# Gathering the whole-array TensorE work of an attention loop in two places per unit, with an earlier start and a mask loaded in pieces

## The chip, the core and the metric

The kernel runs on one core of a Trainium2 chip, in fp32, as one launch. The metric is the time of one execution in microseconds (us), measured on the device. Engine names: PE is TensorE's matmul queue, PEld its weight loads, DVE is VectorE, ACT ScalarE, POOL GpSimd, SP the queue that issues transfers.

## The reference, cut to what matters

```python
def _L0_gnn_ref(features, A, ...):              # a graph layer over 2048 nodes
    A_hat = (A + I) * dinv[:, None] * dinv[None, :]
    agg = einsum('nm,bmd->bnd', A_hat, features)
    h   = relu(batchnorm(agg @ W1.T + b1))
    return batchnorm(h @ W2.T + b2)
def _L1_gnn_ref(h, W, adj):                     # masked attention, 4 heads of 64
    q, k, v = split(h @ W)
    scores  = q @ k.T / sqrt(64) + where(adj == 0, -inf, 0)
    return softmax(scores) @ v
x = layernorm(x + _L0_gnn_ref(x, adj, ...))     # x is (8, 2048, 256)
x = layernorm(x + _L1_gnn_ref(x, W, adj))
```

## The kernel before

Everything up to the second linear layer (1423 us) stays as it is, except for the place of two loads. The change is in attention, which is organised in 64 *units*: 8 batches, 2 pairs of heads, 4 chunks of 512 query rows. A unit has 8 *steps*. In each step a score group S and a weighing group W run:

```python
def scores(u, g):                       # S: 4 matmuls, each on 64 of the 128 rows
    for j in range(g * GJ, (g + 1) * GJ):
        ps = ps_s.tile([P, 2, CH], F32, name="ps_s")         # pool of 2 buffers
        for h in range(2):
            nc.tensor.matmul(ps[:, h, :], kt[hs, ...], qt[hs, ...], ...)
    for j in ...:
        pt = ap_.tile([P, 2, CH], F32, name="pt", bufs=10)
        nc.vector.tensor_tensor(pt, ps, mask[...], op=ALU.subtract)  # frees ps_s
        nc.scalar.activation(pt, pt, AF.Exp, scale=2.0**MASK_EXP)
        nc.gpsimd.tensor_add(acc, acc, pt)                   # sums of the softmax
def weigh(u, g):                        # W: 4 matmuls, each on 64 of the columns
    nc.tensor.matmul(outs[u][h * HD : (h + 1) * HD, :], v[...], pt[:, h, :], ...)
```

About S: its two buffers come free only when DVE has subtracted the mask.

Beside S and W there is *whole-array* work, on all 128 rows and columns: transposes of y and x, the projections to q, k and v, and the transposes that finish a unit. Their results share a pool of two buffers, `ps_m`. There are two layer norms per chunk and batch, one for the input of attention (`prep_norm`) and one for the output (`emit`). Both use this function:

```python
def layernorm(t):
    for i in range(TPC):
        nc.vector.bn_stats(st[:, i, :], t[:, i, :])
        nc.vector.bn_aggr(mv[:, i, :], st[:, i, :])
    nc.vector.tensor_scalar(rs, mv[:, :, 1], EPS, None, op0=ALU.add)      # DVE
    nc.gpsimd.tensor_tensor(rs, rs, mhalf[:, :TPC], op=ALU.pow)           # POOL
    nc.vector.scalar_tensor_tensor(                                       # DVE
        nm, mv[:, :, 0], -1.0, rs, op0=ALU.mult, op1=ALU.mult)
    for i in range(TPC):
        nc.scalar.activation(t[:, i, :], t[:, i, :], AF.Identity,
                             bias=nm[:, i : i + 1], scale=rs[:, i : i + 1])
```

DVE works in order. Between its second-last and its last operation here it has to wait for POOL, which has a queue of 128x1024 additions of its own.

The steps of the whole-array work are set by a table `side`; S and W come from the loop:

```python
for g in range(total + NG):
    scores(g)
    side[(g, 0)]
    weigh(g - LAG)                      # LAG = 2
    side[(g, 1)]
```

This order is not yet the order of the queue: a scheduler may move instructions among each other by its own estimates, unless an instruction is held with `tc.keep_in_program_order`.

Of the kernel before, what the change touches and what calls it, by code (L numbers as in the profile page):

```python
# [8 lines left out]
F32 = mybir.dt.float32  # L9
# [19 lines left out]
def tile_gcn_then_masked_attention(  # L29
# [15 lines left out]
    nc = tc.nc  # L45
    PSUM = bass.MemoryType.PSUM
    P = 128
    B, N, D = x.shape
# [3 lines left out]
    NT = N // P  # L52
    ND = D // P
    NH = H // P
    NO = O // P
    CH = 512
    NCH = N // CH
# [14 lines left out]
    mask_d = dram.tile([P, NT, N], U8, name="mask_d")  # L72
# [21 lines left out]
    with ExitStack() as kept:  # L94
# [182 lines left out]
        with tc.tile_pool(name="l0b", bufs=3) as lp, tc.tile_pool(  # L277
            name="psy", bufs=4, space=PSUM
        ) as psy:
            for i in range(NALL):  # L280
                h = hp_.tile([P, NH, CH], F32, name="h")
                nc.sync.dma_start(h, h_d[i])
                if i == 4:
                    nc.sync.dma_start(wq, wqkv.rearrange("(c p) f -> p c f", p=P))
                    nc.sync.dma_start(mask, mask_d)
                for f in range(NH):
                    nc.scalar.activation(  # L287
                        h[:, f, :], h[:, f, :], AF.Relu,
                        bias=sh1[:, f : f + 1], scale=sc1[:, f : f + 1],
                    )  # L290
                y = lp.tile([P, NO, CH], F32, name="y")
                for o in range(NO):
                    py = psy.tile([P, CH], F32, name="py")
                    for f in range(NH):
                        nc.tensor.matmul(  # L295
                            py,
                            w2s[:, f, o * P : (o + 1) * P],
                            h[:, f, :],
                            start=(f == 0),
                            stop=(f == NH - 1),  # L300
                        )
                    nc.vector.tensor_scalar(y[:, o, :], py, b2s[:, o : o + 1], None, op0=ALU.add)
                    nc.vector.bn_stats(st2[:, o, i, :], y[:, o, :])
                nc.sync.dma_start(y_d[i], y)
            batchnorm_affine(lp, st2, NO, g2s, be2s, sc2, sh2, "2")
# [4 lines left out]
def attention(tc, x, out, adj, mask, wq, ident, ones, mhalf, sc2, sh2, sall, y_d, x1_d):  # L310
# [16 lines left out]
    with ExitStack() as ctx:  # L327
# [28 lines left out]
            return src[b, k * CH : (k + 1) * CH, :].rearrange("(t p) d -> p t d", p=P)  # L356

        def prep_load(b, k):
            yt[b, k] = ap_.tile([P, NO, CH], F32, name="yt")
            nc.sync.dma_start(yt[b, k], y_d[b * NCH + k])  # L360
            x1[b, k] = ap_.tile([P, TPC, D], F32, name="x1", bufs=7)
            nc.sync.dma_start(x1[b, k], rows(b, k, x))
# [20 lines left out]
        def prep_norm(b, k):  # L383
            yt.pop((b, k))
            layernorm(x1[b, k])
            r0 = b * N + k * CH
            nc.sync.dma_start(
                x1_d[r0 : r0 + CH, :].rearrange("(t p) d -> p t d", p=P), x1[b, k]
            )
# [10 lines left out]
        def project(b, hp, c, which):  # L400

            if (b, hp) not in qkv:
                qkv[b, hp] = (
                    ap_.tile([P, N], F32, name="qt"),
                    ap_.tile([P, N], F32, name="kt"),
                    ap_.tile([P, NT, P], F32, name="v"),
                )
            xt = x1t[b]
            cols = slice(c * CH, (c + 1) * CH)
            wcols = slice(which * D + hp * P, which * D + (hp + 1) * P)  # L410
            pm = ps_m.tile([P, CH], F32, name="pm")
            if which < 2:
                for d in range(ND):
                    nc.tensor.matmul(  # L414
                        pm, wq[:, d, wcols], xt[:, d, cols], start=(d == 0), stop=(d == ND - 1)
                    )
                scale = HD**-0.5 * 2.0**-MASK_EXP if which == 0 else 1.0
                nc.scalar.activation(qkv[b, hp][which][:, cols], pm, AF.Copy, scale=scale)
            else:
                for j in range(TPC):  # L420
                    t = c * TPC + j
                    for d in range(ND):
                        nc.tensor.matmul(
                            pm[:, j * P : (j + 1) * P],
                            xt[:, d, t * P : (t + 1) * P],
                            wq[:, d, wcols],
                            start=(d == 0),
                            stop=(d == ND - 1),
                        )
                nc.scalar.copy(  # L430
                    qkv[b, hp][2][:, c * TPC : (c + 1) * TPC, :].rearrange("p t d -> p (t d)"), pm
                )
# [95 lines left out]
                nc.sync.dma_start(rows(b, k, out), t)  # L528


        per_b = HP * NCH * NG
        side = {}

        def at_step(g, s, f, *args):
            side.setdefault((g, s), []).append((f, args))

        def prep_at(b, k, g):
            at_step(g - 6, 0, prep_load, b, k)
            at_step(g - 2, 1, prep_bn, b, k)
            at_step(g, 0, prep_res, b, k, 0)  # L540
            at_step(g, 1, prep_res, b, k, 1)
            at_step(g, 1, prep_norm, b, k)
            for d in range(ND):
                at_step(g + 4, d, prep_t, b, k, d)

        for b in range(B):
            g0 = b * per_b
            for c in range(NCH):
                for w in range(3):
                    at_step(g0 + 3 + 3 * c + w, 1, project, b, 1, c, w)  # L550
            if b + 1 < B:
                for k, g in enumerate((17, 23, 29, 48)):
                    prep_at(b + 1, k, g0 + g)
                for c, g in enumerate((35, 41, 47, 54)):
                    for w in range(3):
                        at_step(g0 + g + 2 * w, 1, project, b + 1, 0, c, w)
        for u in range(len(units)):
            g0 = (u + 1) * NG
            at_step(g0 + 1, 1, finish_copy, u)
            at_step(g0 + 4, 0, finish_sums, u)  # L560
            at_step(g0 + 5, 0, finish, u)
            at_step(g0 + 5, 1, emit, u)

        for k in range(NCH):
            prep_load(0, k)
            prep_bn(0, k)
            for half in range(2):
                prep_res(0, k, half)
            prep_norm(0, k)
            for d in range(ND):  # L570
                prep_t(0, k, d)
            for w in range(3):
                project(0, 0, k, w)

        total = len(units) * NG
        LAG = 2
        for g in range(total + NG):
            if g < total:
                scores(*divmod(g, NG))
            for f, args in side.get((g, 0), ()):  # L580
                f(*args)
            if 0 <= g - LAG < total:
                weigh(*divmod(g - LAG, NG))
            for f, args in side.get((g, 1), ()):
                f(*args)


# [207 lines left out]
```

## Time and profile before

| | before |
|---|---|
| time, median of three executions | 4072.41 us (4071.86 to 4076.46) |
| busy share of PE, DVE, ACT, POOL | 97%, 46%, 41%, 56% |
| first y-transpose to last matmul | 1423.1 to 4066.2 us |
| a steady batch of attention | 324 us |

### The profile page before, as it was taken

What the parts mean: (1) busy time and instruction counts of PE and PEld (TensorE: products, weight loads), DVE (VectorE), ACT (ScalarE), POOL (GpSimd) and SP (SyncE); (2) the same over time, 40 slices, a digit from 0 to 9 for tenths busy, and PEclk for the clock granted to TensorE, in tenths of its full rate; (3) what the DMA queues carried; (4) which work ended last, traced back from release to release, by engine and by line L of the source; (5) the groups of instructions that cost most, each with busy time, mean ns of one, the idle gap of its engine ahead of it and who ended that gap; (6) DMA issues with size and microseconds to landing.
All of it is one profiled execution on the core that took longest, in us unless ns stands there. A gap on an engine that the chain in (4) does not pass through costs nothing. (4 is left out here: it accounts for less than half of the span.)

```text
span 4072.3 us, 38096 instructions
## 1 busy us (share of the span) xinstructions
PE 3938.3 (97%) x14626; PEld 1559.8 (38%) x14626; DVE 1867.2 (46%) x2525; ACT 1665.7 (41%) x2077; POOL 2285.9 (56%) x1083
## 2 busy tenths in 40 slices
PE   7999999999989989999999999999999999999997
PEld 5444444444434433333333333333333333333332
DVE  5211111111124435665565665665656666556565
ACT  5000000000024345555555555555555555545554
POOL 0011101110100038887887887888888888788897
PEclk8999999999999989999999999999999999999998
DMA  5111101110147620000010000000000000000000
GB/s 217 64 45 52 52 31 49 47 49 31 47 158 230 208 68 21 25 28 26 16 42 21 21 32 21 32 32 21 32 21 32 26 27 27 26 6 26 6 1 22
DMA packets 94426, 197.28 MB, mean 48 GB/s; under 512 B 7072, under 2 KB 73120, under 8 KB 83872
## 3 DMA queue, kind: packets, MB, share of 16 engines
q1 hardware_dynamic: 94240, 194.80, 13.7%
q8 instruction: 117, 1.92, 0.2%
q14 instruction: 69, 0.57, 0.0%
HBM read 106.70 MB, written 88.08 MB: 48 GB/s over the span
## 5 line engine op out<-in xcount | busy, mean ns | idle before, releaser
L466 POOL TENSOR_TENSOR acc<-acc,pt 128x1024 f32<-128x1024 f32 x768 | 1814.2, 2362 | 329.1 <-ACT pt L459 286.5
L453 DVE TENSOR_TENSOR pt<-ps_s,mask 128x1024 f32<-128x1024 f32 x1024 | 1209.4, 1217 | 943.5 <-PE ps_s L446 908.4
L459 ACT ACTIVATE pt<-pt 128x1024 f32<-128x1024 f32 x1024 | 1066.5, 1054 | 816.7 <-DVE pt L453 796.2
L446 PE MATMUL ps_s<-qt,kt 64*128 64x512 f32 x4096 | 1041.1, 620 | 47.8 <-DVE pt L453 47.7
L475 PE MATMUL ps_o<-pt,v 128*64 128x512 f32 x4096 | 1013.0, 607 | 2.9 <-ACT pt L459 2.9
L209 PE MATMUL pa<-at,xb 128*128 128x512 f32 x2048 | 885.5, 592 | 0.0
L446 PEld LDWEIGHTS ps_s<-qt,kt 64*128 64x128 f32 x4096 | 351.3, 186 | 640.1 <-issue 339.9
L187 POOL TENSOR_SCALAR xb<-xb,dinv 128x256 f32<-128x256 f32 x112 | 103.0, 948 | 863.9 <-DMA xb<-in_x_dram 851.8
L209 PEld LDWEIGHTS pa<-at,xb 128*128 128x128 f32 x2048 | 389.0, 190 | 487.2 <-issue 480.0
L475 PEld LDWEIGHTS ps_o<-pt,v 128*64 128x64 f32 x4096 | 252.0, 136 | 637.6 <-issue 539.8
L242 ACT ACTIVATE h<-ph,b1s 128x512 f32<-128x512 f32 x128 | 87.9, 687 | 993.9 <-PE ph L235 993.9
L228 DVE TENSOR_TENSOR ag<-pa,dbc 128x512 f32<-128x512 f32 x64 | 44.3, 692 | 769.8 <-PE pa L209 769.8
L464 POOL TENSOR_TENSOR acc<-pt 128x1024 f32<-128x1024 f32 x128 | 302.3, 2362 | 71.4 <-ACT pt L459 70.2
L414 PE MATMUL pm<-x1t,wq 128*128 128x512 f32 x512 | 255.7, 624 | 0.5 <-ACT x1t L398 0.5
L295 PE MATMUL py<-h,w2s 128*128 128x512 f32 x512 | 223.6, 599 | 13.7 <-ACT h L287 13.7
L235 PE MATMUL ph<-ag,w1s 128*128 128x512 f32 x512 | 225.1, 592 | 0.0
L88 POOL TENSOR_TENSOR rs<-rs,mhalf 128x4 f32<-128x4 f32 (+1 forms) x2 | 1.7, 870 | 378.9 <-DVE rs L87 378.9
L350 ACT ACTIVATE x<-x,ln_nm,ln_rs 128x256 f32<-128x256 f32 x256 | 132.6, 588 | 100.0 <-DVE ln_nm L346 100.0
L243 DVE BATCH_NORM_STATS2 st<-h 128x6 f32<-128x512 f32 x128 | 88.8, 694 | 148.5 <-ACT h L242 148.5
L414 PEld LDWEIGHTS pm<-x1t,wq 128*128 128x128 f32 x512 | 88.4, 191 | 165.7 <-issue 104.9
L295 PEld LDWEIGHTS py<-h,w2s 128*128 128x128 f32 x512 | 98.4, 193 | 138.9 <-issue 119.1
L287 ACT ACTIVATE h<-h,sh,sc 128x512 f32<-128x512 f32 x128 | 93.3, 801 | 134.9 <-DMA h<-h_d 125.3
(78 smaller groups left out, 1780.7 us busy)
## 6 DMA issues: line engine op xcount, KB each, us to landing
h_d<-h SPq DMA_DIRECT2D x32, 1024.0 KB, 3.9
h<-h_d SPq DMA_DIRECT2D x32, 1024.0 KB, 5.9
a<-in_adj_dram SPq DMA_DIRECT2D x16, 1024.0 KB, 8.3
xb<-in_x_dram SPq DMA_DIRECT2D x32, 512.0 KB, 3.9
y_d<-y SPq DMA_DIRECT2D x32, 512.0 KB, 6.4
yt<-y_d SPq DMA_DIRECT2D x32, 512.0 KB, 3.3
x<-in_x_dram SPq DMA_DIRECT2D x32, 512.0 KB, 3.8
x_d<-x SPq DMA_DIRECT2D x32, 512.0 KB, 2.8
```

The source lines that it names most:

```text
L187: nc.gpsimd.tensor_scalar(t4[:, j, :], t4[:, j, :], dv, None, op0=ALU.mult)
L209: nc.tensor.matmul(pa, xs[b][m // TPC][:, m % TPC, d * P : (d + 1) * P], at[:, m, c * CH : (c + 1) * CH], start=(m == 0), stop=(m == NT - 1),)
L235: nc.tensor.matmul(ph, w1s[:, d, f * P : (f + 1) * P], ag[:, d, :], start=(d == 0), stop=(d == ND - 1),)
L295: nc.tensor.matmul(py, w2s[:, f, o * P : (o + 1) * P], h[:, f, :], start=(f == 0), stop=(f == NH - 1),)
L350: nc.scalar.activation(t[:, i, :], t[:, i, :], AF.Identity, bias=nm[:, i : i + 1], scale=rs[:, i : i + 1],)
L414: nc.tensor.matmul(pm, wq[:, d, wcols], xt[:, d, cols], start=(d == 0), stop=(d == ND - 1))
L446: nc.tensor.matmul(ps[:, h, :], kt[hs, j * P : (j + 1) * P], qt[hs, k * CH : (k + 1) * CH], start=True, stop=True,)
L453: nc.vector.tensor_tensor(pt, pss[j - g * GJ], mask[:, j, None, k * CH : (k + 1) * CH].to_broadcast([P, 2, CH]), op=ALU.subtract,)
L459: nc.scalar.activation(pt, pt, AF.Exp, scale=2.0**MASK_EXP)
L464: nc.gpsimd.tensor_add(accs[u, q], probs[u, j - 1], pt)
L466: nc.gpsimd.tensor_add(accs[u, q], accs[u, q], pt)
L475: nc.tensor.matmul(outs[u][h * HD : (h + 1) * HD, :], qkv[b, hp][2][:, j, h * HD : (h + 1) * HD], pt[:, h, :], start=(j == 0), stop=(j == ...
```

## The change

A change of the array's shape costs time (0.15 to 0.20 us here, measured in the prediction), and before, whole-array work stands in 366 places of the matmul queue, for 512 steps. The change puts all of it at two steps of each unit, 2 and 5. It also starts the first unit after the first chunk is ready instead of after all four, and loads the mask in 16 pieces. The core of the diff (cuts marked with `...`):

```diff
-                if i == 4:
+                if i == 2:
                     nc.sync.dma_start(wq, ...)
-                    nc.sync.dma_start(mask, mask_d)
+                if 4 <= i < 4 + NT:
+                    nc.sync.dma_start(mask[:, i - 4, :], mask_d[:, i - 4, :])
...
-            yt[b, k] = ap_.tile([P, NO, CH], F32, name="yt")
+            yt[b, k] = ap_.tile([P, NO, CH], F32, name="yt", bufs=3)
...
-                for w in range(3):
-                    at_step(g0 + 3 + 3 * c + w, 1, project, b, 1, c, w)
-            if b + 1 < B:
-                for k, g in enumerate((17, 23, 29, 48)):
-                    prep_at(b + 1, k, g0 + g)
-                for c, g in enumerate((35, 41, 47, 54)):
-                    for w in range(3):
-                        at_step(g0 + g + 2 * w, 1, project, b + 1, 0, c, w)
+                u0 = g0 + c * per_u
+                if b or c:
+                    for w, g in enumerate((2, 2, 5)):
+                        at_step(u0 + g, project, b, 1, c, w)
+                if b + 1 < B:
+                    u0 = g0 + (NCH + c) * per_u
+                    prep_at(b + 1, c, u0 - 3, u0 + 2)
+                    for w, g in enumerate((2, 2, 5)):
+                        at_step(u0 + g, project, b + 1, 0, c, w)
...
+        first_rows(0)
+        first_rows(1)
+        prep_load(0, 3)
+        first_columns(0)
+        at_step(0, first_rows, 2)
+        at_step(1, first_columns, 1)
+        at_step(2, first_rows, 3)
+        at_step(3, first_columns, 2)
+        at_step(5, first_columns, 3)
...
             if g < total:
                 scores(*divmod(g, NG))
-            for f, args in side.get((g, 0), ()):
-                f(*args)
             if 0 <= g - LAG < total:
                 weigh(*divmod(g - LAG, NG))
-            for f, args in side.get((g, 1), ()):
+            for f, args in side.get(g, ()):
                 f(*args)
```

`prep_at(b + 1, c, u0 - 3, ...)` puts the input layer norm at step 5 of the unit before, the same step at which `finish` and `emit` (the output layer norm) stand.

More of the change, by code (lines that the diff above doesn't have):

```diff
@@ L528, in emit, with at_step, prep_at @@
                 nc.sync.dma_start(rows(b, k, out), t)
+        per_u = NG
         per_b = HP * NCH * NG
         side = {}
-        def at_step(g, s, f, *args):
-            side.setdefault((g, s), []).append((f, args))
-        def prep_at(b, k, g):
-            at_step(g - 6, 0, prep_load, b, k)
-            at_step(g - 2, 1, prep_bn, b, k)
-            at_step(g, 0, prep_res, b, k, 0)
-            at_step(g, 1, prep_res, b, k, 1)
-            at_step(g, 1, prep_norm, b, k)
+        def at_step(g, f, *args):
+            side.setdefault(g, []).append((f, args))
+        def prep_at(b, k, g, t):
+            at_step(g - 6, prep_load, b, k)
+            at_step(g - 2, prep_bn, b, k)
+            for half in range(2):
+                at_step(g, prep_res, b, k, half)
+            at_step(g, prep_norm, b, k)
             for d in range(ND):
-                at_step(g + 4, d, prep_t, b, k, d)
+                at_step(t, prep_t, b, k, d)
         for b in range(B):
@@ L548, in attention, with first_rows @@
             for c in range(NCH):
-                for w in range(3):
-                    at_step(g0 + 3 + 3 * c + w, 1, project, b, 1, c, w)
-            if b + 1 < B:
-                for k, g in enumerate((17, 23, 29, 48)):
-                    prep_at(b + 1, k, g0 + g)
-                for c, g in enumerate((35, 41, 47, 54)):
-                    for w in range(3):
-                        at_step(g0 + g + 2 * w, 1, project, b + 1, 0, c, w)
+                u0 = g0 + c * per_u
[7 more added lines that the diff above has]
+                        at_step(u0 + g, project, b + 1, 0, c, w)
         for u in range(len(units)):
             g0 = (u + 1) * NG
-            at_step(g0 + 1, 1, finish_copy, u)
-            at_step(g0 + 4, 0, finish_sums, u)
-            at_step(g0 + 5, 0, finish, u)
-            at_step(g0 + 5, 1, emit, u)
-        for k in range(NCH):
-            prep_load(0, k)
+            at_step(g0 + 1, finish_copy, u)
+            at_step(g0 + 4, finish_sums, u)
+            at_step(g0 + 5, finish, u)
+            at_step(g0 + 5, emit, u)
+        def first_rows(k):
             prep_bn(0, k)
@@ L569, in attention, with first_columns @@
             prep_norm(0, k)
+        def first_columns(k):
             for d in range(ND):
@@ L573, in attention @@
                 project(0, 0, k, w)
+        for k in range(3):
+            prep_load(0, k)
+        first_rows(0)
[7 more added lines that the diff above has]
+        at_step(5, first_columns, 3)
+        for w in range(3):
+            at_step(7, project, 0, 1, 0, w)
         total = len(units) * NG
```

## The prediction

> **What bounds the kernel now.** I read the page first (busy shares, costliest groups), then the timeline of the matmul queue in a steady stretch, then the few places where that queue waits. On the page the columns of a group are line, engine, operation, tiles, shapes, count, then busy us, mean ns of one, and idle time before with its releaser:
>
> ```profile
> PE 3938.3 (97%) x14626; PEld 1559.8 (38%) x14626; DVE 1867.2 (46%) x2525; ACT 1665.7 (41%) x2077; POOL 2285.9 (56%) x1083
> ...
> L466 POOL TENSOR_TENSOR acc<-acc,pt 128x1024 f32<-128x1024 f32 x768 | 1814.2, 2362 | 329.1 <-ACT pt L459 286.5
> ...
> L446 PE MATMUL ps_s<-qt,kt 64*128 64x512 f32 x4096 | 1041.1, 620 | 47.8 <-DVE pt L453 47.7
> L475 PE MATMUL ps_o<-pt,v 128*64 128x512 f32 x4096 | 1013.0, 607 | 2.9 <-ACT pt L459 2.9
> L209 PE MATMUL pa<-at,xb 128*128 128x512 f32 x2048 | 885.5, 592 | 0.0
> ```
>
> TensorE is 97% busy and waits 48 us for score buffers in 4072, so the time is the sum of what its in-order queue holds. The change leaves everything before the second linear layer alone. What it moves lies in attention: from the first y-transpose at 1423.1 us to the last matmul at 4066.2, 2643 us. A steady stretch of the matmul timeline (start us, length us, engine, line, ...):
>
> ```profile
> 2000.63 1.99 PE L446 MATMUL ps_s<-qt,kt 64*128 64x512 f32 x8
> 2002.55 1.94 PE L475 MATMUL ps_o<-pt,v 128*64 128x512 f32 x8
> 2004.41 2.05 PE L423 MATMUL pm<-wq,x1t 128*128 128x128 f32 x16
> 2006.39 1.99 PE L446 MATMUL ps_s<-qt,kt 64*128 64x512 f32 x8
> ```
>
> Read start to start, since the ends are modelled. A score group S (four matmuls, eight records) takes 1.92 us, a weighing group W 1.86, a v projection 1.98. Inside S and W the records of the trace come in pairs 7 ns apart, a new pair every 0.423 us: two 64-row (or 64-column) halves of the array work at once. At every change of shape the gap is 0.52 instead of 0.423, and the second step after it is 0.10 late too (0.05 for W and transposes). A change therefore costs 0.15 to 0.20 us. That is the cost which the change wants to save.
>
> **What the Trainium skill says.** "TensorEngine Tiling (Array Packing)", section Key Properties: changing the tiling mode, not just the tile, drains TensorE. The trace agrees: 0.52 against 0.423 us. "TensorE: Matmul & The Clock Gate", Part 3, section The mechanism: matmuls on different tiles overlap, each starting about 4 ns after the last; here 7 ns. The same section, "What overlaps and what doesn't": matmuls stay in strict order. So a half-array matmul that has no partner next to it in the queue gets none. This case shows that too, in the start of attention:
>
> ```profile
> 1482.76 1.12 PE L446 MATMUL ps_s<-qt,kt 64*128 64x512 f32 x2
> 1483.81 0.66 PE L379 MATMUL pm<-ident,yt 128*128 128x128 f32 x4
> 1484.40 1.98 PE L446 MATMUL ps_s<-qt,kt 64*128 64x512 f32 x6
> 1486.31 1.94 PE L475 MATMUL ps_o<-pt,v 128*64 128x512 f32 x8
> ```
>
> Four transposes stand after the first score matmul of a group. The single one takes 1.05 us, the remaining three 1.91: 2.96 for what costs 1.92 whole. A split score group costs 1.04 us, besides the 0.15 of another whole-array run.
>
> **The change, part by part.** The source puts the projections, transposes and finishing work at steps 2 and 5 of each eight-step unit. But the scheduler that orders the queue makes something else of it. I counted runs of equal shape in the order of both built programs, from the first y-transpose on.
>
> Whole-array runs: 366 before, 249 after. The removed 117, at 0.15 to 0.20 each and with the matmuls themselves unchanged, take the sum of these runs from 509.0 to 488.7 us: -20.3.
>
> Weighing groups: before, 493 whole, 16 of one, 16 of three; after, 505 whole and some eight odd ones. With 1.867, 1.003 and 1.86 us that is 971.5 against 958.2: -13.3.
>
> Score groups: before, 507 whole, 6 of one, 2 of three, 1 of two, 1 of six; after, 423 whole, 115 of one, 59 of three, 28 of two, 1 of eight. 507 x 1.918 + 6 x 1.053 + 2 x 1.91 + 1.06 + 2.78 = 986.4; 423 x 1.918 + 115 x 1.053 + 59 x 1.91 + 28 x 1.06 + 3.64 = 1078.4: +92.0. The reason stands in the order itself: the sequence is v projection and sum transposes, one score matmul, output transposes, three score matmuls. The pool of these results has two buffers, the third piece has to wait for an evacuation, and the scheduler fills its estimated wait with one score matmul of the next step. The same comes between the x transposes and the q and k projections.
>
> The 64 sum groups (1.0 us each) stay. Together 2530.7 before, 2589.0 after: **+58 us** on the queue that sets the end. The working is checked by the kernel before: 2643.1 measured less 2530.7 leaves 112.4 us of waits and cold clock, and comparing each group's own time with its cost puts 26 of them before 1508 us, 29 after 3950 and 57 between.
>
> Mask in pieces. In the second linear layer one stretch stands out:
>
> ```profile
> 1181.92 22.56 PE L295 MATMUL py<-h,w2s 128*128 128x512 f32 x48 [5.38 <-ACT h L287]
> 1212.81 3.59 PE L295 MATMUL py<-h,w2s 128*128 128x512 f32 x4 [8.32 <-ACT h L287]
> ```
>
> The wait is 8.5 us beyond a normal step and the next four matmuls run at 0.85 instead of 0.43 us (the clock gate; "TensorE: Matmul & The Clock Gate", Part 1, The two states you'll see, gives half rate after about 3.4 us idle, and the trace agrees). Together 10 us. In the order of the SyncE queue, the mask load and three y stores stand before the next h loads; the records show the DMA rings at a tenth of their time from 1200 to 1206. In the changed order h loads alternate with stores and pieces. In 6.9 us an iteration then moves 1.5 MB plus 0.25 to 0.75 MB of mask, within the 422 GB/s seen at 1182 to 1188. So all 10 us go: **-10**.
>
> Start of attention. 26 us beyond the groups' cost lie there, 10.6 of them the first chunk's chain, which stays. With three y buffers the third load no longer waits for the first chunk (ACT waits 16.7 us for a y load before), and score groups exist to fill the later layer norms. I take half: **-12**. The part of the last batch in which TensorE waits for POOL shrinks, as projections now lie in four of its units and not in two: an estimate of **-5**.
>
> New waits. DVE also runs the layer norm, in order, and one of its steps waits for a POOL power that queues behind 2.36 us additions:
>
> ```profile
> 1931.85 1.02 POOL L345 TENSOR_TENSOR ln_rs<-ln_rs,mhalf 128x4 f32<-128x4 f32 x1
> 1932.91 0.16 DVE L346 SCALAR_TENSOR_TENSOR ln_nm<-ln_mv,ln_rs 128x4 f32<-128x4 f32 x1 [2.31 <-POOL ln_rs L345]
> 1932.99 3.67 DVE L453 TENSOR_TENSOR pt<-ps_s,mask 128x1024 f32<-128x1024 f32 x3
> 1933.11 2.07 ACT L350 ACTIVATE x<-x,ln_nm,ln_rs 128x256 f32<-128x256 f32 x4 [1.41 <-DVE ln_nm L346]
> 1934.26 1.13 PE L446 MATMUL ps_s<-qt,kt 64*128 64x512 f32 x4 [2.08 <-DVE pt L453]
> ```
>
> DVE stood 2.3 us, and the matmuls 2.1. Such waits sum to about 6 us a batch in eight layer norms. The change puts two layer norms (the next batch's input and this batch's output) in one step, twice a batch; there the row of DVE work between two score evacuations is about 3 us longer. I add 2 x 1.5 us for seven batches, about **+20**.
>
> Sum: 4072 + 58 - 10 - 12 - 5 + 20 = 4123. The last term may fall away, since the broken pairs give DVE more time, so I set 4119.
>
> **Rivals.** First, the intent holds: the runs merge as the source says, 2 per unit, 128 instead of 366, at 0.17 us some 40 us saved, and with the start and the mask 4010. Against it stands the built order, with 249 runs and 87 broken score groups. Second, the broken pairs cost nothing, because the array would wait in those places anyway: then -34 of merging and -27 elsewhere remain, about 4010 to 4030. Against it: in steady state before, waits are only 57 of 2440 us, and a whole-array piece there waits for no evacuation. Third, POOL or DVE becomes the bound: POOL works 272 of 324 us per batch and DVE 197, so an average does not bind, but long whole-array runs starve both and the additions then lag; with 5 us more per unit in 28 preparing units 4230. Against it: ten probability buffers and a lag of two steps cover 8 us, more than the longest such place (transposes, one score, two projections: 1.0 + 1.1 + 3.6).
>
> **Range and chances.** The +58 is counts times durations that repeat to 10 ns; I trust it to 10. The uncertain terms are the waits (0 to 45) and the start and end (-30 to 0). That gives 4080 to 4160. The 2% line is at 4154 on the slow side and 3991 on the fast one. I give faster 0.02, within 2% 0.84, slower 0.14.
>
> **What would show it.** In the timeline of the changed kernel: score rows of x2 and x6 records around the transposes, taking 1.05 and 1.91 start to start; the sum of L447 (scores) groups about 92 us up; whole-array rows about 20 down; no gap near 1204 us; an end of the second linear layer some 10 us earlier. It is wrong if single score matmuls take half a microsecond, or if the steady batch (324 us now) does not become some 7 to 10 us longer.

## More of the kernel before

A busy share of 56% for POOL and 46% for DVE looks harmless. It says nothing, though, of a single place where DVE stands behind POOL. Three rows of the view of waits (engine, line and tile, what it waited for: us in total, times, longest us) show how often this happens before the change:

```profile
ACT x L350 <- DVE ln_nm L346: 100.0, 49, 6.0
DVE ln_nm L346 <- POOL ln_rs L345: 57.0, 35, 4.7
PE ps_s L446 <- DVE pt L453: 47.7, 46, 5.2
```

DVE stands 57 us for POOL's power, up to 4.7 us at a time, and PE stands 48 us for DVE.

## The result, and the profile after

| | before | after |
|---|---|---|
| time, median of four executions | 4074.35 us (4071.86 to 4076.46) | 4236.02 us (4235.21 to 4237.76) |
| ratio | | 1.0398, 95% interval 1.038 to 1.0416 |
| attention starts | 1423.1 us | 1414.0 us |
| first y-transpose to last matmul | 2643.1 us | 2815.1 us |
| of it: count of the queue | 2530.7 us | 2589.0 us |
| of it: the rest (waits and cold clock) | 112.4 us | 226.1 us |
| a steady batch | 324 us | 348 us |

(A ratio here is the mean time of one kernel's fast runs over that of the other's in the same rounds, so it is not quite the ratio of the medians that stand beside it.) The change makes the kernel 4% slower: +162 us where the prediction said +47. "Count of the queue" is the prediction's own sum, group by group in the built order times the measured duration of such a group. I call what the stretch is longer than that its *rest*. The bookkeeping closes: -9.1 (start of attention) + 58.3 (count) + 113.7 (rest) = +162.9.

The page of the kernel after, its engines and then the groups (line, engine, operation, tiles, shapes, count, then busy us, mean ns, idle before and its releaser):

```profile
PE 4042.7 (95%) x14626; PEld 1590.1 (38%) x14626; DVE 1853.0 (44%) x2525; ACT 1694.5 (40%) x2077; POOL 2284.2 (54%) x1083
...
L467 POOL TENSOR_TENSOR acc<-acc,pt 128x1024 f32<-128x1024 f32 x768 | 1812.3, 2360 | 462.4 <-ACT pt L460 421.3
...
L447 PE MATMUL ps_s<-qt,kt 64*128 64x512 f32 x4096 | 1178.5, 642 | 115.4 <-DVE pt L454 114.2
L476 PE MATMUL ps_o<-pt,v 128*64 128x512 f32 x4096 | 1006.0, 611 | 4.1 <-ACT pt L460 4.1
```

All work counts are the same, and no engine does more of anything, yet PE's score group grew by 137 us of busy time and its wait for DVE from 48 to 114. Both are marks of trouble: the busy time grows with broken groups (92 us in the prediction's sum), and also where the matmuls run at half the clock, as shown below. The same rows of the view of waits as before:

```profile
ACT x L351 <- DVE ln_nm L347: 156.3, 63, 6.3
PE ps_s L447 <- DVE pt L454: 114.2, 62, 5.5
DVE ln_nm L347 <- POOL ln_rs L346: 110.9, 64, 3.6
```

DVE's wait for POOL's power has doubled, and it now happens in all 64 layer norms. The timeline of one place (start us, length us, engine, line, ...) shows what it does; both layer norms of a step lie just here:

```profile
2055.38 0.16 DVE L345 TENSOR_SCALAR ln_rs<-ln_mv 128x4 f32<-128x4 f32 x1
2055.56 2.36 POOL L467 TENSOR_TENSOR acc<-acc,pt 128x1024 f32<-128x1024 f32 x1 [0.85 <-ACT pt L460]
2056.58 1.94 PE L476 MATMUL ps_o<-pt,v 128*64 128x512 f32 x8
2057.88 1.01 POOL L346 TENSOR_TENSOR ln_rs<-ln_rs,mhalf 128x4 f32<-128x4 f32 x1
2058.86 2.33 POOL L467 TENSOR_TENSOR acc<-acc,pt 128x1024 f32<-128x1024 f32 x1
2058.92 2.30 DVE L347 SCALAR_TENSOR_TENSOR ln_nm<-ln_mv,ln_rs 128x4 f32<-128x4 f32 x1 [3.38 <-POOL ln_rs L346]
2061.14 2.34 DVE L454 TENSOR_TENSOR pt<-ps_s,mask 128x1024 f32<-128x1024 f32 x2
2062.41 3.78 PE L447 MATMUL ps_s<-qt,kt 64*128 64x512 f32 x8 [3.90 <-DVE pt L454]
```

Read it from the DVE rows. DVE hands `rs` to POOL at 2055.54. POOL has just begun an addition of 2.36 us and comes to the power only at 2057.88. So DVE stands 3.38 us. Its next operation handles 128x4 elements and takes 0.16 us elsewhere, but here it takes 2.30: it starts 0.06 us after POOL's next addition and ends with it. The Trainium skill says why, in "SBUF — State Buffer", section Who interferes with whom: a DVE instruction with two inputs in SBUF contends with a GpSimd instruction that reads SBUF, and the one that comes second is blocked for the whole length of the other. The trace agrees, 2.30 beside 2.33 us. Together DVE gives no score buffer back for 5.7 us, and PE stands 3.90 us; then its score group of 1.92 us takes 3.7, up to the next group at 2066.12. Nothing holds this group in its middle: the second subtraction ends at 2063.48, and the second half starts at 2064.27, in step with the rest. From its second pair on, the matmuls of this group start 0.85 us apart instead of 0.43: the granted clock is one half from 2061.04 to 2067.87. The view of stretches (us, busy time of each engine, granted clock, DMA share, GB/s) shows it:

```profile
2061.00:2068.00 7.00, 5.59 (x14) 1.78 (x16) 4.93 (x5) 5.19 (x8) 2.82 (x3) 0.51 0.26 79
```

So this stand is paid twice. From the first y-transpose on, PE has 6 waits of over 3 us before and 21 after; in each of the 27 cases the clock is at half when PE goes on, or within 3.5 us. There are 7 stretches at half the clock before (49 us) and 27 after (138 us). PE was busy in 34 us of them before and in 122 after. An estimate from these figures: half of that time is lost, 17 us before and 61 after.

By comparing each S and W group with its own cost, the waits between S and W are 67.8 us in the whole run before and 182.4 after. That is +114.6, which is all of the growth of the rest; what else is in it stayed, 44.6 and 43.7. What I call waits here is a group's time beyond its cost, so the slow groups after a wait are in it: PE's idle time in this part of the kernel grew by 67 us (86.5 to 153.4), and the half clock accounts for about 44 by the estimate above. In a steady batch they sit at four places: two steps with both layer norms (6.4 to 7.4 us each) and two with an output layer norm alone (3.4 and 4.9).

One more thing changed, and it is in DVE's queue. The place of a single output layer norm in the kernel before:

```profile
2443.82 0.17 DVE L344 TENSOR_SCALAR ln_rs<-ln_mv 128x4 f32<-128x4 f32 x1
2443.90 1.22 DVE L453 TENSOR_TENSOR pt<-ps_s,mask 128x1024 f32<-128x1024 f32 x1
2445.12 2.32 DVE L346 SCALAR_TENSOR_TENSOR ln_nm<-ln_mv,ln_rs 128x4 f32<-128x4 f32 x1
```

Here a mask subtraction stands between the two small operations, so DVE frees a score buffer while POOL takes the power, and it has no wait. That is so in 38 of the 64 layer norms before and in none after. In the trace after, such a place (2497 us) has 0.86 + 1.13 + 2.30 us of these operations and DVE's wait in one piece. From 1704 to 3792 us, 6 of the intervals between two subtractions hold more than 3 us of this before and 24 after: 12 with 4.3 us, 12 with 5.8. No run keeps the subtraction in its place in the gathered schedule.

Now what the prediction did see. A broken score group after the change, in the same view:

```profile
2141.99 1.12 PE L447 MATMUL ps_s<-qt,kt 64*128 64x512 f32 x2
2143.04 0.66 PE L518 MATMUL pm<-ident,ot 128*128 128x128 f32 x4
2143.63 1.98 PE L447 MATMUL ps_s<-qt,kt 64*128 64x512 f32 x6
2145.54 1.94 PE L476 MATMUL ps_o<-pt,v 128*64 128x512 f32 x8
```

Start to start the parts take 1.05 and 1.91, so the group takes 2.96 instead of 1.92, in steady state as it did at the start before. And the stretch of the second linear layer that held the two waits:

```profile
1182.38 43.00 PE L296 MATMUL py<-h,w2s 128*128 128x512 f32 x94 [5.37 <-ACT h L288]
```

It is one row now: the 8.32 us wait is gone.

### The profile page after: what moved, and what is told of

Read it like the earlier page. It is cut to its first block, busy times and chain, and to the rows that moved or that the text cites. A ratio compares the mean times of both kernels' runs of the same rounds, so it can differ in the third digit from the quotient of the medians.

```text
span 4235.0 us, 38139 instructions
## 1 busy us (share of the span) xinstructions
PE 4042.7 (95%) x14626; PEld 1590.1 (38%) x14626; DVE 1853.0 (44%) x2525; ACT 1694.5 (40%) x2077; POOL 2284.2 (54%) x1083
## 3 DMA queue, kind: packets, MB, share of 16 engines
q8 instruction: 117, 1.92, 0.2%
## 5 line engine op out<-in xcount | busy, mean ns | idle before, releaser
L447 PE MATMUL ps_s<-qt,kt 64*128 64x512 f32 x4096 | 1178.5, 642 | 115.4 <-DVE pt L454 114.2
L476 PE MATMUL ps_o<-pt,v 128*64 128x512 f32 x4096 | 1006.0, 611 | 4.1 <-ACT pt L460 4.1
L447 PEld LDWEIGHTS ps_s<-qt,kt 64*128 64x128 f32 x4096 | 378.5, 190 | 771.3 <-DVE pt L454 391.5
L228 DVE TENSOR_TENSOR ag<-pa,dbc 128x512 f32<-128x512 f32 x64 | 44.3, 692 | 771.1 <-PE pa L209 771.1
L415 PE MATMUL pm<-x1t,wq 128*128 128x512 f32 x512 | 240.0, 612 | 4.6 <-ACT x1t L399 4.6
L235 PEld LDWEIGHTS ph<-ag,w1s 128*128 128x128 f32 x512 | 97.2, 190 | 122.7 <-issue 122.0
```

The lines of the kernel that those rows point to most:

```text
L235: nc.tensor.matmul(ph, w1s[:, d, f * P : (f + 1) * P], ag[:, d, :], start=(d == 0), stop=(d == ND - 1),)
L415: nc.tensor.matmul(pm, wq[:, d, wcols], xt[:, d, cols], start=(d == 0), stop=(d == ND - 1))
L447: nc.tensor.matmul(ps[:, h, :], kt[hs, j * P : (j + 1) * P], qt[hs, k * CH : (k + 1) * CH], start=True, stop=True,)
L476: nc.tensor.matmul(outs[u][h * HD : (h + 1) * HD, :], qkv[b, hp][2][:, j, h * HD : (h + 1) * HD], pt[:, h, :], start=(j == 0), stop=(j == ...
```

## The experiments

Two theories stood after the result. **DVE-stand**: the missing 114 us come from DVE standing in the layer norm in steps where no whole-array matmuls lie beside it any more. **Structure**: they come from the gathered schedule itself, that is long runs of whole-array work that wait for the evacuation of their two buffers or starve the other engines. Twelve kernels were run, in three calls of four, each with three rounds; the kernel before had medians of 4074.6, 4074.4 and 4074.5 us in them. For each I give the median, the ratio to before, and "count / rest" as defined above.

### e1_mask: the mask pieces alone

```diff
 (kernel before)
-                if i == 4:
+                if i == 2:
                     nc.sync.dma_start(wq, ...)
-                    nc.sync.dma_start(mask, mask_d)
+                if 4 <= i < 4 + NT:
+                    nc.sync.dma_start(mask[:, i - 4, :], mask_d[:, i - 4, :])
```

> The kernel before with the mask loaded in 16 pieces and wq two iterations earlier, and nothing else of the change. If the 8.5 us wait at 1204 us and the four cold matmuls after it come from that load and the order of the SyncE queue around it, the time falls by 9 to 10 us, to about 4064, and attention starts 9 us earlier. Rival: the h loads are short of bandwidth there and wait anyway; then it stays at 4074.

Measured: 4063.39 us (4061.01 to 4064.30), ratio 0.9972 (0.9955 to 0.9989), 2530.7 / 112. Attention starts at 1412.8 instead of 1423.1. The mask part is worth the 10 us that were predicted.

### e2_spread: the new start and the mask, with the old steady schedule

```diff
 (kernel before, with the edit of e1_mask)
+            yt[b, k] = ap_.tile([P, NO, CH], F32, name="yt", bufs=3)
-        for k in range(NCH):
-            prep_load(0, k) ... prep_bn, prep_res, prep_norm, prep_t, project
+        first_rows(0); first_rows(1); prep_load(0, 3); first_columns(0)
+        at_step(0, 1, first_rows, 2) ... at_step(5, 1, first_columns, 3)
```

> The changed kernel's mask pieces, three y buffers and start of attention, but the steady schedule of before (whole-array work spread over the steps). Theory: the whole loss of 162 us lies in the steady schedule; then this kernel is 10 to 20 us faster than before, 4052 to 4064. Rival: the new start, where the first unit competes with the preparation, has a part in the loss; then it is slower than 4074.

Measured: 4059.41 us (4056.95 to 4061.81), ratio 0.9961 (0.9945 to 0.9978), 2526.6 / 113.6. The start gives 4 us on top of the mask, about as much as the spread of either kernel's runs; by the trace all of it is in the count, and no wait was saved. The whole loss of the kernel after therefore lies in its steady schedule: 4236.02 - 4059.41 = 177 us.

### e3_pin: the intended order, without broken groups

```diff
 (kernel after)
-                    nc.tensor.matmul(          # in scores and in weigh
+                    mm = nc.tensor.matmul(
                         ...
                     )
+                    tc.keep_in_program_order(mm)
```

> The changed kernel with score and weighing matmuls held in the source's order, so that the built order has 130 whole-array runs and no broken score group (2470 us of matmul queue by my count against 2589). Theory of the broken groups: the 119 us go, less 30 to 50 us of new waits for evacuations inside the longer runs: 4145 to 4170. If the layer-norm waits on DVE are a separate cost, the waits for DVE in the steps after the finishing work stay. Rival: a single score matmul only fills time in which the array would wait for the evacuation anyway; then within 20 us of 4236.

Measured: 4254.63 us (4253.25 to 4256.96), ratio 1.0441 (1.0424 to 1.0459), 2470.4 / 365.1. The expectation missed. The order is what the source intends: 130 runs of whole-array work and no broken group, 119 us less in the count than after. The rest grows by 139 us all the same, to S and W waits of 252 us and about 79 us in the midst of the long whole-array runs. The view of waits of this kernel:

```profile
PE ps_s L447 <- DVE pt L455: 166.6, 89, 5.5
PE pm L415 <- ACT x1t L399: 20.3, 33, 6.0
```

So breaking the groups is not what makes PE wait. The broken pieces seem rather to have hidden some of DVE's standing, but the hold moved DVE's operations too (14 layer norms have a subtraction in their middle again), so this is not shown. Both theories stay alive: the first row grew, which is DVE-stand, and there are waits for evacuations, which is Structure.

### e4_emit9: the output layer norm at another step

```diff
 (kernel after)
-            at_step(g0 + 5, emit, u)
+            at_step(g0 + 9, emit, u)
```

> The changed kernel with only the output layer norm of a unit moved four steps later, from step 5 (just after the whole-array work) to step 1 (just before it); the same number of runs and broken groups. Theory of cover: DVE's layer-norm chain is hidden only when whole-array work stands beside it; the waits for DVE fall from 22 us a batch to under 8, time 4236 - 7.5 x 15 = about 4120. Rival: a layer norm costs its wait wherever it stands, because DVE stops for POOL; then within 20 us of 4236.

Measured: 4224.03 us (4221.54 to 4225.93), ratio 1.0368 (1.0350 to 1.0385), 2589.0 / 214, and the result is wrong. The last unit's `emit` falls beyond the end of the loop, so the last chunk is never written. Nor did the run test anything: the built order has the layer norm in the same place as before, since the scheduler moved the DVE operations forward to where their data was ready. It says nothing for either theory.

### f1_chain: no step of the layer norm for which DVE waits

```diff
 (kernel after, in layernorm)
-            nc.vector.tensor_scalar(rs, mv[:, :, 1], EPS, None, op0=ALU.add)
+            nc.gpsimd.tensor_scalar(rs, mv[:, :, 1], EPS, None, op0=ALU.add)
             nc.gpsimd.tensor_tensor(rs, rs, mhalf[:, :TPC], op=ALU.pow)
-            nc.vector.scalar_tensor_tensor(
-                nm, mv[:, :, 0], -1.0, rs, op0=ALU.mult, op1=ALU.mult)
+            nc.gpsimd.tensor_tensor(nm, mv[:, :, 0], rs, op=ALU.mult)
+            nc.gpsimd.tensor_scalar(nm, nm, -1.0, None, op0=ALU.mult)
```

POOL does the whole chain now, so DVE passes on to the next mask subtraction at once, and only ACT waits.

> The changed kernel with the three small operations of a layer norm between its statistics and its scaling (add eps, power, minus mean times scale) all on POOL, so that DVE waits for POOL nowhere in it[...]. Built matmul order as in the changed kernel (2590 us by count). Theory: the waits of the matmul queue come from DVE standing in these operations (26.6 us a batch in the changed kernel); then the waits between score and weighing groups, 182 us, fall under 70, time about 4120. Rival: DVE's own statistics work without whole-array work beside it is what costs; then it stays above 4200.

Measured: 4092.93 us (4091.59 to 4093.54), ratio 1.0045 (1.0028 to 1.0062), 2589.7 / 82. The schedule of the matmuls is as after, the count the same, and 143 us are gone. The view of waits:

```profile
PE ps_s L446 <- DVE pt L453: 9.3, 18, 0.6
```

From 114 to 9 us, the longest from 5.5 to 0.6. Of the 182 us of S and W waits 42 remain. Structure alone, with nothing altered in the gathered schedule, could not give this. Of the 143 us, 84 are PE's idle time (153.4 to 69.3) and about 53 the half clock, by the same estimate (busy in it for 122 us, now for 17).

### f2_spread_chain: the same chain in the old schedule

```diff
 (e2_spread, with the edit of f1_chain in layernorm)
```

> The same on the kernel with the changed start and mask and the steady schedule of before (4059). It has 70 us of such waits; if DVE's standing is their cause 35 to 50 us go, 4010 to 4025. Rival: POOL, at 84% in a batch and now with 2 to 3 us more a layer norm, becomes late itself; then 4059 or more.

Measured: 4035.78 us (4034.88 to 4037.57), ratio 0.9905 (0.9888 to 0.9921), 2526.5 / 88, and the result is right. This beats both kernels, by 1% the one before. The chain is worth 24 us here and 143 us in the gathered schedule. The kernels f1 and f2 have nearly the same rest (82 and 88), so their difference, 57 us, measures the two matmul orders (the broken groups less the merged runs); their counts differ by 63.

### f3_pin_chain: the intended order with the chain on POOL

```diff
 (e3_pin, with the edit of f1_chain in layernorm)
```

> The same on the kernel with matmuls held in the source's order (4255, 2470 us by count, 365 us of waits of which 252 between score and weighing groups). If DVE's standing is the cause these fall under 100, time about 4100. If even so more than 200 us stay, the long whole-array runs starve the chain of score, mask, exp and sum by themselves, and the time stays above 4200.

Measured: 4084.00 us (4083.20 to 4084.77), ratio 1.0024 (1.0007 to 1.0041), 2470.4 / 191. The chain takes 171 us off e3_pin. But Structure is not nothing: 76 us of S and W waits remain and the 79 us within the long whole-array runs did not move. The count is 56 us lower than in f2_spread_chain, the rest 103 higher. So the change's aim, fewer changes of shape, loses in this form even when its two side effects are taken away.

### f4_late: DVE stands as long, but beside whole-array work

```diff
 (kernel after)
-                nc.vector.bn_stats(st[:, i, :], t[:, i, :])
+                bs = nc.vector.bn_stats(st[:, i, :], t[:, i, :])
+                if held:                       # in emit only
+                    tc.keep_in_program_order(bs)
-            at_step(g0 + 5, emit, u)
+            at_step(g0 + 10, emit, u)
-        for g in range(total + NG):
+        for g in range(total + NG + 4):
```

The output layer norm comes at step 2 of the next unit, where projections lie, and is held there.

> The changed kernel with the output layer norm emitted at step 2 of the unit after next and its statistics held in that place of DVE's order, so that it stands beside the transposes and projections of that step (the run before this, moved four steps in the source alone, was still hoisted by the scheduler to where it had been). Same matmul order as the changed kernel. Theory of cover: the waits of its four places a batch, 22 us, fall to under 5, time about 4100. Rival: the layer norm stops DVE for POOL wherever it is and the score groups wait the same; then 4216 to 4256.

Measured: 4113.06 us (4110.83 to 4115.16), ratio 1.0097 (1.0080 to 1.0114), 2589.0 / 100; 39 of the rest lie at the end, where the last layer norms now stand alone. It is 123 us faster than after, at the same count. And DVE stands longer, not shorter. The group of the last layer norm operation in this kernel (the number after the bar is busy us, then mean ns, then idle before):

```profile
L349 DVE SCALAR_TENSOR_TENSOR ln_nm<-ln_mv,ln_rs 128x4 f32<-128x4 f32 x64 | 19.0, 297 | 182.3 <-POOL ln_rs L348 182.3
```

Wait and operation together are 201 us here and 190 after (78.8 + 110.9), while PE's wait for DVE is 41 us instead of 114. One place in its timeline shows the reason:

```profile
2131.61 2.31 PE L417 MATMUL pm<-x1t,wq 128*128 128x512 f32 x5
...
2132.20 0.17 DVE L347 TENSOR_SCALAR ln_rs<-ln_mv 128x4 f32<-128x4 f32 x1
...
2133.84 1.99 PE L449 MATMUL ps_s<-qt,kt 64*128 64x512 f32 x8
2135.76 1.94 PE L478 MATMUL ps_o<-pt,v 128*64 128x512 f32 x8
...
2138.06 0.16 DVE L349 SCALAR_TENSOR_TENSOR ln_nm<-ln_mv,ln_rs 128x4 f32<-128x4 f32 x1 [5.69 <-POOL ln_rs L348]
...
2139.42 2.26 PE L449 MATMUL ps_s<-qt,kt 64*128 64x512 f32 x8 [1.72 <-DVE pt L456]
```

DVE stands 5.69 + 0.16 us, as long as in the place of the kernel after (3.38 + 2.30). But when it stops, PE still has a projection to finish before its next score group. It loses 1.8 us before the following group and 0.3 in it, instead of 3.9 and 1.8; its wait is too short here to cost it the clock. In this run the half clock holds PE's work for 28 us instead of 122. Two things besides the place changed. The collision is nearly gone (19.0 us busy instead of 78.8), though the sum of DVE's stand is the same. And the input and output layer norms no longer share a step. No run parts this from the cover; if each of the two shared places had cost only what an output layer norm alone cost after, 3.4 to 4.9 us, about 5 us a batch would be saved, of some 15, by an estimate from the four places above.

### e7_port: only the collision of the last operation taken away

```diff
 (kernel after, in layernorm; minus is a 128x1 tile of -1.0)
-            nc.vector.scalar_tensor_tensor(
-                nm, mv[:, :, 0], -1.0, rs, op0=ALU.mult, op1=ALU.mult)
+            for i in range(TPC):
+                nc.vector.tensor_scalar(
+                    nm[:, i : i + 1], mv[:, i, 0:1], rs[:, i : i + 1], minus,
+                    op0=ALU.mult, op1=ALU.mult)
```

Each of the four operations streams one tensor; the second factor is a scalar per partition. The wait for POOL's power stays.

> The changed kernel with one small DVE operation of the layer norm (minus mean times scale, two tensors from memory, 2.30 us in half of its 48 cases between 1704 and 3792 us, 0.16 in the others) replaced by four that read one tensor and per-partition scalars; the power stays on POOL. If the 2.30 us is a wait for the memory port that POOL's addition holds and only two-tensor operations take it, the long cases vanish and 40 to 60 us go: 4180 to 4195. Rival: one-tensor operations wait for it as well, or the wait for the power is what counts; then 4220 to 4250.

Measured: 4175.86 us (4175.10 to 4177.68), ratio 1.0249 (1.0232 to 1.0266), 2589.0 / 167.6. The same group after, and in this kernel:

```profile
L347 DVE SCALAR_TENSOR_TENSOR ln_nm<-ln_mv,ln_rs 128x4 f32<-128x4 f32 x64 | 78.8, 1232 | 110.9 <-POOL ln_rs L346 110.9
```

```profile
L350 DVE TENSOR_SCALAR ln_nm<-ln_mv,ln_rs,minus 128x1 f32<-128x1 f32 x256 | 52.4, 267 | 111.2 <-POOL ln_rs L348 111.2
```

No operation of 2.30 us is left; the longest of the 256 takes 0.275, though 194 of them start within a POOL addition. The wait for POOL is the same 111 us. So the collision is worth 60 of the 143 us that the chain is worth: PE's idle time falls by 30, and its busy time at half the clock from 122 to 50 us, about 36 more. The rest goes with the wait for POOL's queue; that is argued by subtraction. One tensor alone does not protect an operation: `ln_rs<-ln_mv`, on one tensor of 128x4, lasts until 0.03 us after the end of POOL's addition in all 22 of its 64 cases here that start within one.

### g1_spread_pin_chain, g3_pin_late, g2_pin_late_chain: combinations

```diff
 g1: (f2_spread_chain, with the edit of e3_pin)
 g3: (kernel after, with the edits of e3_pin and f4_late)
 g2: (kernel after, with the edits of e3_pin, f4_late and f1_chain)
```

> Changed start and mask, steady schedule of before, layer-norm operations on POOL, and matmuls held in the source's order, which joins the 14 broken weighing groups and some transposes: 2507 us by count against 2526 in the run without the hold (4036). If the hold costs nothing here, since whole-array work is in short pieces, about 4017, the fastest kernel. Rival: held matmuls wait for evacuations as in the other held kernels (79 us there); then 4036 or more.

Measured: 4041.44 us (4039.54 to 4042.88), ratio 0.9920 (0.9903 to 0.9937), 2507.3 / 112. Holding the order in the old schedule takes 19 us from the count and adds 24 to the rest. The scheduler's small disorder there is not a loss.

> The held kernel with only the output layer norm moved beside whole-array work, its operations still shared by DVE and POOL. Held alone it took 4255 with 252 us of waits between score and weighing groups. Theory of cover: four of six layer-norm places a batch are repaired, 130 to 160 us go: 4095 to 4125. Rival: in the held order the layer norms of the inputs cost as much; then above 4180.

Measured: 4108.76 us (4105.81 to 4110.94), ratio 1.0082 (1.0065 to 1.0099), 2470.4 / 219. The waits between S and W fall from e3_pin's 252 to 100 us.

> The intent of the change with both repairs: matmuls held in the source's order (130 whole-array runs, no broken group, 2470 us by count), output layer norm beside whole-array work, its small operations on POOL. The held kernel with POOL operations alone waits 191 us (4084), of it 76 between score and weighing groups and 79 inside the long whole-array runs. Theory: the layer-norm part, about 45 of the 76, goes, the evacuation waits stay: about 4040, so that the merging pays no better than spreading. Rival: evacuation waits shrink too once ACT and DVE are freer; then under 4015.

Measured: 4069.67 us (4068.46 to 4070.39), ratio 0.9989 (0.9972 to 1.0005), 2470.4 / 177. This missed the expectation by 30 us. It is the best of the gathered kernels and no better than before. The waits inside the whole-array runs stay, and with the chain on POOL the layer norm's scaling on ACT comes late, as the view of waits shows:

```profile
ACT x L352 <- POOL ln_nm L350: 438.0, 62, 12.2
```

ACT, also in order, stands up to 12.2 us behind POOL's additions, and ACT is the engine that evacuates the projections. That the two belong together is argued from the lines, not shown by a run of its own; the fastest kernel, f2_spread_chain, has the same wait at 280.6 us.

## Why the prediction was wrong, step by step

**The bound and the count of the queue: right.** TensorE's queue is what sets the end, and its count grew by 58 us. f1_chain and f2_spread_chain, which differ in the schedule and have nearly the same rest, are 57 us apart.

**Whole-array runs -20.3 and weighing groups -13.3: the right direction.** On the page the q and k projections fall from 255.7 to 240.0 us of busy time and the x transposes from 44.3 to 36.0, with the other whole-array groups within 3 us; the weighing groups fall by 7 (1013.0 to 1006.0). These are not start-to-start times, so the terms are confirmed only within the sum. (The weighing counts that the prediction lists for before add up to 966.2; its 971.5 has in it one run of three groups at the end, which is not listed.)

**Mask -10: right.** Attention starts 9.1 us earlier after the change and 10.3 in e1_mask.

**Start -12: mis-sized.** The first part's rest went from 26 to 23 us. In e2_spread the new start gave 4 us, from fewer changes of shape and not from waits.

**End -5: not seen.** The wait for POOL that was to shrink is only 1.9 us before; it is gone after. In the last 116 us of the matmul queue PE waits 24.5 us before and 27.6 after.

**New waits "about +20": this step failed.** The rest between start and end went from 57 to 183 us, +126. Two things were wrong in it. First, "there the row of DVE work between two score evacuations is about 3 us longer. I add 2 x 1.5 us for seven batches" counted only the steps with two layer norms. The steps with one output layer norm cost 3.4 and 4.9 us too. Second, I took half of DVE's longer work as hidden. I had sized the cost of DVE's standing from the kernel before, and I read the built order of the matmul queue but not that of DVE's. DVE's own standing grows only by about 6 us per batch (20.7 to 26.6, its two small layer norm operations, with the waits before them), but PE's standing grows by 16, of which the half clock is about 5 by the estimate above. Three things made the same standing dearer:

- It comes in longer pieces. A subtraction stood in the middle of 38 of the 64 layer norms before, and of none after.
- Less lies beside it. In the changed kernel the places that cost fall into steps of S and W alone, of 1.92 + 1.86 = 3.78 us; three of the eight layer norms of a steady batch before had a projection of about 1.9 us beside them and cost PE nothing. But this is not the whole difference: the other five had no whole-array matmul beside their small operations either (counted from 1.5 us before to 1.2 after them), and cost 0.7 to 3.9 us each.
- The longer waits of PE are followed by half the clock. PE was busy in it for 12 us between start and end before and for 90 after, which makes about 39 us of the 126.

f1_chain (DVE doesn't stand: -143 us) and f4_late (it stands as long, in long pieces, beside whole-array work: -123 us) show that DVE's standing is the cause and that cover takes most of it away. How much of the growth is DVE's order and how much the missing cover stays open.

The mechanism itself was in the prediction, with a trace of it: DVE waits for POOL's power behind additions. The half clock was in it too, for the second linear layer, but not for these waits. What was missing was the collision of the 128x4 operation with POOL's addition. It was in the trace before, with a mean of 969 ns for an operation that takes 0.16 us alone, and I did not look at that mean. e7_port puts 60 us on it in the kernel after. It did not grow in sum, though: the two small operations are busy for 47.5 + 62.0 us before and 27.9 + 78.8 after.

Two of the prediction's own signs show it as well: the steady batch became 24 us longer instead of 7 to 10, and the scores line grew by 137 us instead of 92.

**"Since the broken pairs give DVE more time" the last term may fall away: wrong in effect.** e3_pin, without broken pairs, does wait more (365 against 226), so the pairs do give DVE time. But they give it at their own place, and the layer norms stand elsewhere.

**The rivals.** The intent (4010) was rightly rejected on the built order, but for a reason that is too narrow. Built as intended, the order gives 4254.63, and 4084.00 with the DVE waits taken out. "POOL or DVE becomes the bound ... 4230" came nearest to the time, by luck (28 times 5 us on the prediction's own sum without its waits, 4103, would be 4243). I dismissed it with "ten probability buffers and a lag of two steps cover 8 us". That looked at the additions lagging behind. The short supply is the two score buffers, which cover no more than the next group.

What stays open: the 76 us of waits between S and W and the 79 us inside the long runs of f3_pin_chain were not traced to one cause each. A third buffer for whole-array results, if room were made for it, would tell whether the second of them is a matter of that pool's depth; I did not try it.

## What to carry to other kernels

Work that seems to cost only changes of shape may at the same time be the cover for another engine's short stands; before gathering it, list for each step how long the in-order engine that frees the next buffer can stand, and what of the bound engine's queue is left beside it. Read the built order of that engine's queue as well: a useful operation between two that wait for each other is cover too. An order in which an engine waits for a second engine and then continues itself (DVE, POOL, DVE) is dear in an in-order queue: give the second engine the rest of the chain if it can do it, which took 143 us off the gathered schedule and made the older one, with the new start, the fastest, at 4035.78 us. Look at the mean of the tiny operations in the list of groups: 969 ns for 128x4 elements is a collision, not a cost.

## What the Trainium skill lacked or had wrong

- "SBUF — State Buffer", section Who interferes with whom, has the exclusive lock right, but no figure for what it does to a small operation. Here a DVE operation on 128x4 elements took 2.30 us instead of 0.16 beside a POOL addition of 2.33 us, in 32 of 64 cases (24 of 64 before), in each case that began within such an addition. Four operations on one tensor of 128x1 with per-partition scalars took 0.267 us each and were never held; one on a tensor of 128x4 was (22 of 64 cases).
- "TensorEngine Tiling (Array Packing)", section Key Properties, says that a change of mode drains TensorE, without a cost. In fp32 with 512 columns it is 0.15 to 0.20 us per change here, about a tenth of a group of 1.92 us.
- "TensorE: Matmul & The Clock Gate", Part 3, section The mechanism, gives about 4 ns between the starts of overlapping matmuls; here, with halves of 64 rows or columns in fp32, it is 7 ns.
